# Both halves of the output projection written to a ring of three PSUM banks

## The chip, the cores and the metric

The kernel runs on one core of a Trainium2 chip. The core has a matrix engine (TensorE, PE in the profile; its weight loads are the row PEld), VectorE (DVE), ScalarE (ACT), GpSimd (POOL) and SyncE (SP), which only issues transfers. Each engine works through its own queue in order, and semaphores make it wait for others. Matrix products can be written only to PSUM, which this program divides into eight banks of 128 x 512 float32. The metric is the device time of one execution in microseconds.

## What is computed

The input is 2 sequences of 2048 rows with 256 channels. Each row goes through a layer norm, and from there two branches start:

- a selective state-space layer (Mamba) with an MLP behind it. In short:

```python
xz = rmsnorm(xn) @ in_proj_w.T;  xp, z = split(xz)
xc = silu(conv4(xp) + conv_b)
dt, Bm, Cm = ...                       # from xc
h = h * exp(dt * A) + (dt * xc) * Bm   # a scan over the sequence, 512 channels x 16 states
y = sum_s(h * Cm) + xc * D
x1 = xn + (y * silu(z)) @ out_proj_w.T
s = x1 + silu(rmsnorm(x1) @ mlp_w1.T) @ mlp_w2.T
```

- a mixture of 8 experts of which each row takes its 2 likeliest: a hidden layer of 1024 with relu, a second product back to 256, weighted and summed, then silu; call it `g`.

The output is `x + s * g`. The step that this document is about is `x1 = xn + (y * silu(z)) @ out_proj_w.T`.

## The kernel before

The 4096 rows are cut into 8 blocks of 512 (c = 0 to 7), the 512 channels into 4 groups of 128 (d = 0 to 3), and the 16 states into 8 pairs (g = 0 to 7). The main loop has 8 x 4 x 8 = 256 steps, one for each (c, d, g). In a step VectorE multiplies the input by B (L1498) and runs two scans of 512 (L1502), ScalarE makes the exponentials two steps ahead (L1387), GpSimd multiplies by C (L1430), in most steps adds the two states of the pair (L1432), and TensorE sums the results into a bank for `y` through an identity matrix (L1400), three steps later.

**A planner in Python writes the order.** Each step has two ticks. In each tick the loop emits its own work, then `later.run()` emits what has come due, then `draw` emits filler work for TensorE worth about 1.93 us. The filler comes from generators in lists of falling rank: `pre`, `zs` (the gate projections of `z`), `projs` (the output projections), `chain` (the projections for the next block) and `side` (the expert and MLP tiles). A generator that yields "wait" is passed over for the rest of the tick, and the next list is asked.

**`later` is a list of work with due times.** `later.put(work, frees, after=n)` puts work, such as the step that empties a PSUM bank, n ticks ahead. Whoever wants a bank calls `bank(tag, ...)`, and that calls `later.free`: if the earlier user of the bank has not yet been emitted to its end, everything due up to that end is emitted now, ahead of its time. The chip's engines then wait for each other by semaphores.

**The banks.** Two banks hold the pair of inputs to the scans, one holds dt x xc, one `y`, one has the tag "o" and three have the tag "h". The single bank "o" holds the second product of an expert or MLP tile, and the output projection. The ring of three, "h", holds the conv inputs (px, L621), the small projections (pxd L666, pd L685), the gate projections (pz, L772), the hidden products of the tiles (phe and phm, L946), the transposes (pxse and pxsm, L934), and the scratch output of the squares (sq, L863).

**Expert and MLP tiles** (`Ffn.run`). A tile makes four pairs of hidden products, then waits for `held` to be empty, takes "o", puts its name into `held`, makes 8 second products (poe or pom, L958), clears `held` and calls `finish`. For an expert `finish` plans one add (ys, L1066) two ticks later. For an MLP tile it plans an add (L1218) and behind it a group of three steps (L1228, L1229, L1230, output xom), for which the tanh of the weighted experts (ScalarE, L1207) must be there; its GpSimd sum (L1203) must come before that. An MLP tile's hidden products go through a silu on ScalarE (hidm, L1144), which needs another table than the exponentials (table loads, L183).

**The output projection** (`out_proj(c)`). It is put into `projs` when block c + 1 begins. It loads two halves of `xn`, waits until the last channel group's gated `y` (the product sz, L1408) has been emitted, and then makes two halves of 16 matmuls each (po, L821). For each half it plans an add (L855, result xnr) two ticks later, two squares (L863) and a store to DRAM (L870). When both are made, `projected` lets the gate projections d = 1 to 3 of the next block go. For block 7 (`last`) the first three channel groups are made ahead of time, the first half in "o" and the second in "h".

Of the kernel before, what the change touches and what calls it, by code (L numbers as in the profile page):

```python
# [14 lines left out]
NB, L, DM = 2, 2048, 256  # L15
# [3 lines left out]
P = 128  # L19
# [9 lines left out]
JS = TS // P  # L29
# [23 lines left out]
def kernel(  # L53
# [126 lines left out]
    def act_table(name):  # L180

        if table[0] != name:
            nc.scalar.preload_act_table_set(name)  # L183
            table[0] = name
# [86 lines left out]
    moff, rstd, both_norms, _, _, off = (stat[:, 2 + n, :] for n in range(6))  # L271
# [88 lines left out]
    def can(tag, bufs):  # L360

        n = count.get(tag, 0)
        return n < bufs or n - bufs in gone.get(tag, ())

    def take(tag):
        n = count[tag] = count.get(tag, 0) + 1
        return n - 1

    def drop(tag, n):
        gone.setdefault(tag, set()).add(n)  # L370
# [3 lines left out]
    held = []  # L374

    def ring(tag, bufs):

        n = take(tag)
        later.free(tag, n - bufs)
        return tag, n  # L380

    def bank(tag, shape, name):
        n = ring(tag, 3 if tag == "h" else 1)
        pool = ps_h if tag == "h" else ps_1
        return pool.tile(shape, F32, tag=tag, name=name), n
# [422 lines left out]
    def out_proj(c):  # L808
        last = c == NBLK - 1
        halves = []  # L810
        for hf in range(2):
            while not can("xs", 2):
                yield "wait"
            nx = take("xs")
            xn = rows.tile([P, JS, DM], F32, tag="xs", name=f"xnr{c}_{hf}")
            nc.sync.dma_start(xn, xnd[c][:, ts(hf, JS), :])
            halves.append((hf, xn, nx))
        def product(po, hf, d):

            for j in range(JS):  # L820
                nc.tensor.matmul(  # L821
                    po[:, j, :], szs[c, d][:, ts(hf * JS + j, P)], ow_sb[:, d, :],
                    start=(d == 0 and j == 0), stop=(d == ND - 1 and j == JS - 1),
                )

        pos = []
        if last:

            while (c, ND - 2) not in y_made or held:
                yield "wait"  # L830
            for hf in range(2):
                pos.append(bank("h" if hf else "o", [P, JS, DM], f"po{c}_{hf}"))
                for d in range(ND - 1):
                    product(pos[hf][0], hf, d)
                yield 3 * MM
        while (c, ND - 1) not in y_made:
            yield "wait"
        for hf, xn, nx in halves:
            while (held and not last) or (last and not can("x1", 2)):
                yield "wait"  # L840
            if last:
                po, n = pos[hf]
                product(po, hf, ND - 1)
            else:
                po, n = bank("o", [P, JS, DM], f"po{c}_{hf}")
                for d in range(ND):
                    product(po, hf, d)
            x1 = xn
            if last:
                n1 = take("x1")  # L850
                x1 = rows.tile([P, JS, DM], F32, tag="x1", name=f"x1l{hf}")
                x1_last.append((x1, n1))

            def add(po=po, xn=xn, x1=x1):
                nc.vector.tensor_tensor(x1, po, xn, ALU.add)  # L855

            def squares(hf=hf, x1=x1):
                if last:
                    act_table(WITH_LN)
                sq, ns = bank("h", [P, JS, DM], f"sq{c}_{hf}")  # L860
                for j in range(JS):
                    i = c * J + hf * JS + j
                    nc.scalar.activation(  # L863
                        sq[:, j, :], x1[:, j, :], AF.Square, accum_out=rms[:, 0, i : i + 1],
                    )
                drop(*ns)

            def store(hf=hf, xn=xn, nx=nx):
                if not last:
                    nc.sync.dma_start(x1d[c][:, ts(hf, JS), :], xn)  # L870
                drop("xs", nx)
                if last:
                    root(c, hf)
                elif hf and c == NBLK - 2:
                    root(c)

            later.put(add, n, after=1 if last else 2)
            later.put(squares, after=2 + hf if last else 3)
            later.put(store, after=3 + hf if last else 4)
            yield MM if last else 4 * MM  # L880
        projected.add(c)

    def root(c, hf=None):

        i0, i1 = (c * J, (c + 1) * J) if hf is None else (c * J + hf * JS, c * J + (hf + 1) * JS)
        engine = nc.gpsimd if hf is None else nc.vector
        ss, ms, r, tmp = (rms[:, n, i0:i1] for n in range(4))
        engine.tensor_scalar(ms, ss, 1.0 / DM, RMS_EPS, ALU.mult, ALU.add)
        act_table(WITH_LN)
        nc.scalar.activation(r, ms, AF.Ln)  # L890
        nc.scalar.activation(r, r, AF.Exp, scale=-0.5)
        newton(engine, r, ms, tmp)
        ready_blocks.update((c, h) for h in range(2) if hf in (None, h))
# [577 lines left out]
    for n in range(NS):  # L1471
        c, d, g = at[n]
# [12 lines left out]
        if c > 0 and d == 0 and g == 0:  # L1485
            projs.append(out_proj(c - 1))
        if n == NS - 4:
            projs.append(out_proj(NBLK - 1))
# [97 lines left out]
```

## Time and profile before

| | |
|---|---|
| median of 3 runs | 1489.96 us (1489.83 to 1492.37) |
| profiled execution | 1505.4 us, its span 1503.7 us |
| mean granted clock of TensorE | 0.944 |
| TensorE busy | 1347.4 us (90%) |
| VectorE busy | 1217.2 us (81%) |
| GpSimd busy | 1188.3 us (79%) |
| ScalarE busy | 978.5 us (65%), of it 121 table loads 155.2 us |
| matmuls of the output projection | 256, 61.0 us |

The output projections of the eight blocks begin at 322.8, 470.8, 635.3, 782.5, 937.0, 1105.7, 1309.5 and 1430.4 us of the span. Expert tiles run from about 165 to 1052 us, MLP tiles from there to the end.

In the lists, a bracket such as `[1.94 <-DVE ys L1066]` means that the engine stood idle for 1.94 us before the instruction, and that the wait was ended by the step on VectorE that wrote `ys`, at line 1066. A timeline gives start and duration of neighbouring instructions of one kind, merged. The granted clock is the share of full speed that TensorE was allowed.

### The profile page before, as it was taken

To read this page: it belongs to the slowest core of one execution; us is meant where nothing else is said; L and a number is where in the kernel's file an instruction comes from. 1 tells how busy PE (TensorE), PEld (TensorE's weight loads), DVE (VectorE), ACT (ScalarE), POOL (GpSimd) and SP (SyncE) were. 2 spreads that over 40 slices of the span, in tenths; PEclk is the share of its full clock that TensorE was granted. 3 is DMA by queue.
4 is the path that set the end of the run, shared out by engine and by line. 5 is a ranking of instruction groups with operands and counts; after the bars stand their busy time and mean duration, and the time that the engine had idled before them with its cause. 6 is when DMAs were issued, how large, how long until landed. Compare 5 with 4: busy or idle time off the path is not lost.

```text
span 1503.7 us, 18025 instructions
## 1 busy us (share of the span) xinstructions
PE 1347.4 (90%) x5122; PEld 944.1 (63%) x5122; DVE 1217.2 (81%) x1351; ACT 978.5 (65%) x1765; POOL 1188.3 (79%) x964
## 2 busy tenths in 40 slices
PE   5744799999999999999999999979878998999958
PEld 4531467765776677766776677546655666667726
DVE  7448888889798998799888988999767967888853
ACT  4742777458655776568656865677648988778932
POOL 2665779987898799968997899889975888777860
PEclk9556899999999999999999999999999999999989
DMA  5568134962477345924492449445830116412110
GB/s 187 198 234 304 46 99 145 306 220 76 125 230 280 92 131 180 335 95 121 158 363 74 129 140 331 167 139 175 268 114 8 55 53 211 139 53 60 57 57 14
DMA packets 169317, 231.85 MB, mean 154 GB/s; under 512 B 19825, under 2 KB 139761, under 8 KB 169217
## 3 DMA queue, kind: packets, MB, share of 16 engines
q1 hardware_dynamic: 163072, 213.91, 42.9%
q0 software_dynamic: 6144, 16.79, 3.4%
q8 instruction: 41, 0.67, 0.2%
q14 instruction: 60, 0.48, 0.1%
HBM read 195.12 MB, written 35.52 MB: 153 GB/s over the span
## 4 chain that ended last, share of the span: by engine, by line
PE 44%; POOL 25%; DVE 10%; ACT 10%; issue 6%; DMA 4%; another core or an unknown queue 1%; POOLq 0%; DVEq 0%; SPq 0%; ACTq 0%
POOL h L1430 13%; PE phe L946 9%; PE y L1400 8%; PE poe L958 8%; POOL h L1432 6%; PE pom L958 4%; PE phm L946 4%; PE po L821 3%; ACT L183 2%; PE px L621 2%; DVE h L1502 2%; DMA B<-bcd 2%; ACT da L1387 2%; PE pz L772 2%; DMA C<-bcd 1%
## 5 line engine op out<-in xcount | busy, mean ns | idle before, releaser
L1430 POOL TENSOR_TENSOR h<-h,C 128x1024 f32<-128x1024 f32 x255 | 604.1, 2371 | 36.7 <-issue 11.5
L1502 DVE TENSOR_TENSOR_SCAN h<-da,hs,b 128x512 f32<-128x512 f32 x384 | 477.6, 1270 | 41.4 <-PE y L1400 10.8
L1387 ACT ACTIVATE da<-dt,a_neg 128x512 f32<-128x512 f32 x512 | 352.8, 717 | 93.3 <-DVE h L1502 87.2
L1400 PE MATMUL y<-h,ident 128*128 128x512 f32 x596 | 307.3, 617 | 34.6 <-POOL h L1432 17.5
L1498 DVE TENSOR_TENSOR b<-du,B 128x1024 f32<-128x1024 f32 x256 | 315.0, 1231 | 18.4 <-DMA B<-bcd 9.1
L1432 POOL TENSOR_TENSOR h<-h 128x512 f32<-128x512 f32 x214 | 275.4, 1287 | 16.8
L946 PE MATMUL phe<-xsTe,w_e 128*128 128x256 f32 (+1 forms) x1248 | 268.1, 366 | 9.4 <-ACT xsTe L937 7.6
L946 PEld LDWEIGHTS phe<-xsTe,w_e 128*128 128x128 f32 x1248 | 225.4, 194 | 72.7 <-issue 27.6
L958 PE MATMUL poe<-w_e,hide 128*128 128x256 f32 x1136 | 265.2, 380 | 2.5 <-ACT hide L1053 2.5
L958 PEld LDWEIGHTS poe<-w_e,hide 128*128 128x128 f32 x1136 | 213.8, 190 | 65.1 <-issue 33.5
L1053 ACT ACTIVATE hide<-phe,b 128x256 f32<-128x256 f32 (+1 forms) x312 | 123.6, 450 | 140.8 <-PE phe L946 140.4
L1400 PEld LDWEIGHTS y<-h,ident 128*128 128x128 f32 x596 | 112.2, 197 | 124.0 <-issue 60.5
L1502 DVE TENSOR_TENSOR_SCAN h<-da,b 128x512 f32<-128x512 f32 x128 | 151.3, 1210 | 12.7 <-PE y L1400 4.8
L183 ACT ACT_TABLE_LOAD x121 | 155.2, 1283 | 2.9 <-PEq L1573 0.8
L946 PE MATMUL phm<-xsTm,w_m 128*128 128x256 f32 x512 | 121.0, 387 | 2.7 <-ACT hidm L1144 2.0
L1424 POOL COPY hs<-h 128x2 f32<-128x2 f32 x192 | 42.0, 219 | 100.9 <-DVE h L1502 89.4
L958 PE MATMUL pom<-w_m,hidm 128*128 128x256 f32 x512 | 121.0, 386 | 0.0
L946 PEld LDWEIGHTS phm<-xsTm,w_m 128*128 128x128 f32 x512 | 99.1, 194 | 29.6 <-issue 10.8
L958 PEld LDWEIGHTS pom<-w_m,hidm 128*128 128x128 f32 x512 | 98.5, 194 | 25.2 <-issue 12.5
L462 POOL DMA_INDIRECT xs_d<-xt,slot x64 | 64.0, 1000 | 49.1 <-issue 21.4
L646 DVE SCALAR_TENSOR_TENSOR xc<-px,par_sb,xc 128x512 f32<-128x512 f32 x96 | 71.6, 748 | 30.4 <-ACT xc L638 25.6
L1185 POOL DMA_INDIRECT yk<-ys_d,row_y x60 | 58.3, 972 | 22.6 <-issue 14.2
(221 smaller groups left out, 1366.7 us busy)
## 6 DMA issues: line engine op xcount, KB each, us to landing
w_e<-in_w SPq DMA_DIRECT2D x312, 256.0 KB
B<-bcd SPq DMA_DIRECT2D x64, 512.0 KB
C<-bcd SPq DMA_DIRECT2D x64, 512.0 KB
xs<-xs_d SPq DMA_DIRECT2D x32, 256.0 KB
ys_d<-ys SPq DMA_DIRECT2D x32, 256.0 KB
b<-in_b SPq DMA_DIRECT2D x39, 128.0 KB
xnr<-xnd SPq DMA_DIRECT2D x16, 256.0 KB
xom<-in_x SPq DMA_DIRECT2D x16, 256.0 KB
```

Of the source, the lines that this page charges most:

```text
L183: nc.scalar.preload_act_table_set(name)
L462: r = nc.gpsimd.indirect_dma_start(out=xs_d, out_offset=bass.IndirectOffsetOnAxis(ap=slot[:, k, i : i + 1], axis=0), in_=x_of(i // J, i % ...
L646: nc.vector.scalar_tensor_tensor(v[:, s : s + T], px, conv_w[:, d, KC - 1 - s : KC - s], v[:, s : s + T], ALU.mult, ALU.add,)
L946: nc.tensor.matmul(ph[:, q, :], self.w1[c0 // 2][:, k, ts(q, P)], self.xT[:, k, :], start=(k == 0), stop=(k == KM - 1),)
L958: nc.tensor.matmul(po[:, j, :], self.hid[c // 2][:, c % 2, ts(j, P)], self.w2[c // 2][:, c % 2, :], start=(c == 0 and j == 0), stop=(c == ...
L1053: nc.scalar.activation(hc[:, q, :], ph[:, q, :], AF.Relu, bias=self.b1[:, c0 + q : c0 + q + 1])
L1387: nc.scalar.activation(das[n][:, q, :], dts[c, d], AF.Exp, scale=a_neg[:, d, 2 * g + q : 2 * g + q + 1])
L1400: nc.tensor.matmul(ys[c, d], ident, hts[n][:, q, :], start=False, stop=(g == DS // 2 - 1 and q == nq - 1),)
L1430: engine.tensor_tensor(hts[n], hts[n], bct[c, "C", g], ALU.mult)
L1432: nc.gpsimd.tensor_tensor(hts[n][:, 0, :], hts[n][:, 0, :], hts[n][:, 1, :], ALU.add)
L1498: nc.vector.tensor_tensor(inp, dus[c, d].unsqueeze(1).to_broadcast([P, 2, T]), bct[c, "B", g], ALU.mult,)
L1502: nc.vector.tensor_tensor_scan(hts[n][:, q, :], das[n][:, q, :], inp[:, q, :], 0.0 if c % CPB == 0 else hs[c - 1][:, d, 2 * g + q : 2 * g ...
```

## The change

In `out_proj` of blocks 0 to 6 both halves ask for a bank of the ring "h" instead of "o", and neither waits for `held` any longer. The lines for block 7 stay: its first half keeps "o", and the wait for `held` ahead of it (L829) is not touched.

```diff
         while (c, ND - 1) not in y_made:
             yield "wait"
         for hf, xn, nx in halves:
-            while (held and not last) or (last and not can("x1", 2)):
+            while last and not can("x1", 2):
                 yield "wait"
             if last:
                 po, n = pos[hf]
                 product(po, hf, ND - 1)
             else:
-                po, n = bank("o", [P, JS, DM], f"po{c}_{hf}")
+                po, n = bank("h", [P, JS, DM], f"po{c}_{hf}")
                 for d in range(ND):
                     product(po, hf, d)
```

## The prediction

> **What bounds the kernel now.** I read the engine totals and the 40 slices first, then the stretches of 50 us, then the TensorE groups, and last the timelines around each output projection.
>
> The totals and the slices of the page:
>
> ```profile
> PE 1347.4 (90%) x5122; PEld 944.1 (63%) x5122; DVE 1217.2 (81%) x1351; ACT 978.5 (65%) x1765; POOL 1188.3 (79%) x964
> ...
> PE   5744799999999999999999999979878998999958
> ```
>
> TensorE is the engine to watch: from slice 6 to the end of the 26th it is a row of nines. The answer by stretches gives 735.87 us busy of the 750 us from 200 to 950 (14.1 us idle in all), and 295.51 of the 314 from 1116 to 1430. In the first of these stages an idle microsecond of TensorE is a microsecond of the end; around 1100 it is one only if nothing else is late.
>
> The groups of TensorE, output projection only (columns: busy us, mean ns | idle us before them, and what ended it):
>
> ```profile
> L821 PE MATMUL po<-ow_sb,sz 128*128 128x256 f32 x256 | 61.0, 393 | 16.4 <-DVE xom L1230 10.6 <-DVE ys L1066 3.5 <-DVE xnr L855 1.6
> ```
>
> All three names are work that empties the single bank: the end of an MLP tile (xom), the end of an expert tile (ys) and the projection's own first half (xnr). The timeline places them by block. Here is block 5, TensorE and then VectorE:
>
> ```profile
> 1095.98 3.62 PE L958 MATMUL pom<-w_m,hidm 128*128 128x256 f32 x16
> 1105.74 5.79 PE L821 MATMUL po<-ow_sb,sz 128*128 128x256 f32 x16 [6.15 <-DVE xom L1230]
> 1112.31 3.72 PE L821 MATMUL po<-ow_sb,sz 128*128 128x256 f32 x16 [0.78 <-DVE xnr L855]
> ```
>
> ```profile
> 1099.64 0.67 DVE L1408 SCALAR_TENSOR_TENSOR sz<-y,sz 128x512 f32<-128x512 f32 x1
> 1100.23 0.69 DVE L1218 TENSOR_TENSOR pom<-pom,x1m 128x512 f32<-128x512 f32 x1
> 1103.37 0.70 DVE L1228 SCALAR_TENSOR_TENSOR pom<-yk,pom 128x512 f32<-128x512 f32 x1 [2.46 <-ACT yk L1207]
> ...
> 1111.57 0.69 DVE L855 TENSOR_TENSOR xnr<-po,xnr 128x512 f32<-128x512 f32 x1 [4.78 <-PE po L821]
> ```
>
> The operand of the projection (sz, L1408) is ready at 1100.3, but the bank only at 1105.6, since asking for it makes the planner put the MLP's four closing steps ahead. Then VectorE itself stands 4.78 us, because the add is put into its queue before the product exists. The same pairs elsewhere on TensorE:
>
> ```profile
> 322.78 3.72 PE L821 MATMUL po<-ow_sb,sz 128*128 128x256 f32 x16 [1.94 <-DVE ys L1066]
> ...
> 470.76 3.72 PE L821 MATMUL po<-ow_sb,sz 128*128 128x256 f32 x16 [0.39 <-DVE ys L1066]
> ...
> 786.93 3.72 PE L821 MATMUL po<-ow_sb,sz 128*128 128x256 f32 x16 [0.78 <-DVE xnr L855]
> ...
> 936.98 3.72 PE L821 MATMUL po<-ow_sb,sz 128*128 128x256 f32 x16 [1.18 <-DVE ys L1066]
> ...
> 1309.54 3.69 PE L821 MATMUL po<-ow_sb,sz 128*128 128x256 f32 x16 [3.21 <-DVE xom L1230]
> ```
>
> Block 2 (635.28) shows no wait. The stall total of blocks 0 to 6 is 1.94 + 0.39 + 0.78 + 1.18 + 6.15 + 0.78 + 3.21 = 14.43 us. The remaining 2 us of the 16.4 are the last block's, which the diff leaves as they are.
>
> **The change part by part.** No instruction is added or taken away: 16 matmuls a half, one add, two squares, one store stay. No DMA is added; the loads of xn are still asked for at the start of out_proj, ahead of the waits. SP's store of the half (L870) waits for the add, and behind it stand the next loads of the MLP (xom at 1117.16 after the store of 1112.29); an earlier add lets them go earlier. GpSimd's queue is passed by nothing. What changes is the place of the two halves in TensorE's queue, and the bank.
>
> *The waits for the bank that go.* What is late next is the operand sz, so each wait is cut only to that. Block 0: sz done at 308.3, all 1.94 goes. Block 1: sz ends at 469.44 + 0.67 = 470.11, TensorE is free at 470.37, all 0.39 goes. Block 3: the second half no longer waits for the first one's add, 0.78 goes. Block 4: sz ends at 936.60 and the products could start at about 936.65 instead of 936.98, 0.33 goes. Block 6: sz ends at 1297.0, TensorE free at 1306.33, all 3.21 goes. Block 5: the first half could start at 1100.45, so 5.29 goes, and 0.78 of the second. Its first half also ran slow: 5.80 us in the chain for 16 matmuls that take 3.72 elsewhere, with a granted clock of 0.67 between 1106 and 1112; 2.08 more if the idle time no longer drops the clock. That makes 8.15. But GpSimd had 10.94 us of work in the 18 us from 1098 to 1116, so no more than 7.06 can be won there before it is the bound; I take 7.0. Sum: 1.94 + 0.39 + 0.78 + 0.33 + 7.0 + 3.21 = 13.65 us.
>
> *VectorE's forced adds.* The idle times of VectorE before these adds and before ys and pom (4.78, 2.46, 4.34 in blocks 5 and 6) go or shrink, because the add now comes two steps of the planner later. In blocks 0 to 4 VectorE is 656 us busy of 750, so I cost this at nothing; cover is TensorE's work, and without that cover it would be a further gain.
>
> *An earlier place.* In blocks 0 and 6 the operand was ready 14 and 12 us before the products began, and the planner held them back until the tile ended. Now they go into the middle of the tile's second products. Total work is unchanged and the tile ends two halves (7.4 us) later, so after it both orders stand at the same place. The three later gate projections pz, which wait for out_proj in the planner, come earlier by the same. What is queued behind: TensorE's next tile, whose weights are loaded ahead. Zero, between -1 and +1 us a block.
>
> *Two more takers of the ring of three.* Only block 7's second half uses this ring in the trace, at a time when little else does, so I bound the cost. From below: nothing, since the first half takes a bank last used by a pair of hidden products or a transpose, already emptied by ScalarE (in block 5: hidm at 1090.62 and the sz step at 1095.17, both before 1100). The fourth product after it, some 3.7 + 1.7 + 1.7 us behind its end, needs its add, which comes two planner steps later (about 4 to 5 us). From above: the longest wait of TensorE for this ring near an out_proj, px for DVE xc L646 at 1144.03, 3.92 us. Nearest row: the first hidden products after block 1's projection, which wait 0.55 us for the squares that use the same ring. I take half of it in each of seven blocks, 1.9 us; ends 0 and 7 x 3.92 = 27.4.
>
> **Sum.** 13.65 - 1.9 = 11.7 us less. The profiled execution was 1505.4 us (span 1503.7), the median is 1489.96, a factor of 0.9897; 1493.7 x 0.9897 = 1478.4 us.
>
> **The rivals.**
>
> *Slower: the ring runs short.* Hidden products, px, pz, pd, transposes, squares and now both halves share three banks. If, in the seven blocks, the product behind the halves must wait for an add or for taps as px did at 1144 (3.92), the loss is 27.4 against 13.65: 1519.2 x 0.9897 = 1503.5 us. It decides from 13.65 / 7 = 1.95 us a block. For it: that wait is real. The clock goes with it: px ran its four matmuls in 3.68 instead of 1.88 us after it, at a granted clock of 0.79 between 1142 and 1150, while the 3.21 us at 1306 were followed by 1.00. The Trainium skill, "TensorE: Matmul & The Clock Gate", "What's actually happening", says that the clock falls to half after about one idle window of 3.4 us and needs about as long at work to return; the trace agrees on both sides of that limit. By this rule each wait of 3.92 would cost another 3.4 / 2 = 1.7 us, an estimate, and this rival would end at 1515.3 us instead of 1503.5; the forecast, whose waits stay under a microsecond, would not move. Against it: 200 to 950 shows TensorE with 14.1 us idle in all, with the squares on this ring already, and the release times above leave some 2 us. The Trainium skill, "Perfetto Trace Analysis", "Optimization Strategy", reads a gap that repeats on the engine that should be busy as a sign that room for the next tile can be short. This rival is that rule turned on the ring of three; in this trace the gap repeats at the single bank, and at the ring it shows 3.92 once, which is why the rival gets less than half the forecast's chance.
>
> *No change.* From 756 on, the chain of waits runs through GpSimd's products more than through TensorE, and after block 5 TensorE stands at 1144 for ScalarE in any case. If blocks 0 to 5 give nothing back and only block 6 does, 3.21 - 1.9 = 1.3 us: 1504.1 x 0.9897 = 1488.7 us.
>
> *More.* No ring wait at all, the full 14.43 + 2.08 = 16.5 us: 1488.9 x 0.9897 = 1473.6 us. Against it: the wait for sz remains in blocks 4 and 5.
>
> **How the numbers follow.** The forecast 0.62, more 0.06, no change 0.12, the short ring 0.20. Faster 0.68, within 0.2% (3 us, about what can be told from no change) 0.12, slower 0.20. The forecast alone reaches from 1474 to 1486 (ring cost 0 to 8). The range takes in the no-change case, most of the larger gain and the first third of the slower case: 1471 to 1496.
>
> **What would show it.** Right: L821 loses xom and ys as releasers except in block 7 (1.19 there stays), the idle before it falls from 16.4 to 2 to 5 us, block 5's halves take 3.7 us each, and the halves of blocks 0 and 6 lie inside a tile's second products. Wrong: the idle before phe, phm, px and pz (9.4, 2.7, 5.9 and 0.7) grows by more than 13 with DVE xnr or ACT sq as releaser. The prediction fails too if GpSimd or ScalarE fills the stretch at 1098 to 1116, so that its 18 us stay.

## The result and the profile after

The changed kernel takes 1477.07 us (median of 4 runs, 1475.81 to 1477.73) against 1491.16 us of before: a ratio of 0.9901, 95% interval 0.9889 to 0.9913. On another chip it was 0.9883 (0.9863 to 0.9903): 1488.6 against 1504.41 us. The ratio is an estimate of its own and not the quotient of the two medians, which would be 0.9906 and 0.9895. The time of the first 110 us differs from chip to chip and from run to run: the first product of the y groups begins at 99.8 us in one trace and at 119.5 in another. So runs on different chips are compared by their ratios here, and traces by markers behind that stretch.

The totals and the slices of the page of the changed kernel:

```profile
PE 1337.3 (91%) x5122; PEld 937.0 (63%) x5122; DVE 1214.0 (82%) x1351; ACT 979.8 (66%) x1767; POOL 1186.6 (80%) x964
...
PE   5843999999999999999999999988898998999958
```

The same number of matmuls, 10 us less of busy time, and a span of 1475.6 instead of 1503.7 us. Of these 28.1 us, 11.2 lie ahead of the first place where the two programs differ. Now TensorE's groups of the changed kernel (busy us, mean ns | idle us before, and what ended it): the output projection, and the takers of the ring that could have inherited its waits.

```profile
L946 PE MATMUL phe<-xsTe,w_e 128*128 128x256 f32 (+1 forms) x1248 | 266.5, 365 | 11.1 <-ACT xsTe L937 7.5 <-ACT hide L1053 2.0 <-DVE xc L646 1.0
L946 PE MATMUL phm<-xsTm,w_m 128*128 128x256 f32 x512 | 121.5, 389 | 4.2 <-ACT hidm L1144 3.5 <-ACT xsTm L937 0.7
L821 PE MATMUL po<-ow_sb,sz 128*128 128x256 f32 x256 | 57.6, 380 | 2.0 <-DVE xom L1230 1.2 <-DVE sz L1408 0.8
L621 PE MATMUL px<-xrTr,in_sb 128*128 128x512 f32 x96 | 47.1, 614 | 5.9 <-DVE xc L646 3.9 <-ACT hide L1053 2.0
L1396 PE MATMUL y<-xc,ddiag 128*128 128x512 f32 x64 | 34.4, 620 | 7.8 <-DVE sz L1408 7.8
```

The 16.4 us before L821 are 2.0, all of it block 7's. Its busy time fell by 3.4 us, 2.4 of it in block 5, where no half runs at a low clock any more (7.07 us for both instead of 5.79 and 3.72). Of the others, phe has 1.7 us more than before (9.4), phm 1.5 more (2.7), px the same 5.9, and the first product of a new y group, which waits for sz, 3.4 more (4.4). A second trace of the same kernel (e0) has phe at 9.9, phm at 2.7 and the y group at 7.4, so of these only the last repeats. It is mostly two new waits, 1.78 and 1.21 us, after projections 0 and 2, which start early. The waits did not simply move to the ring.

Block 5 on TensorE, and on VectorE, in the changed kernel:

```profile
1081.87 3.62 PE L958 MATMUL pom<-w_m,hidm 128*128 128x256 f32 x16
1085.32 7.07 PE L821 MATMUL po<-ow_sb,sz 128*128 128x256 f32 x32
1092.23 1.02 PE L1396 MATMUL y<-xc,ddiag 128*128 128x512 f32 x2
```

```profile
1085.57 0.67 DVE L1408 SCALAR_TENSOR_TENSOR sz<-y,sz 128x512 f32<-128x512 f32 x1
...
1087.34 0.67 DVE L1218 TENSOR_TENSOR pom<-pom,x1m 128x512 f32<-128x512 f32 x1
...
1090.48 0.67 DVE L855 TENSOR_TENSOR xnr<-po,xnr 128x512 f32<-128x512 f32 x1
1091.06 0.68 DVE L1228 SCALAR_TENSOR_TENSOR pom<-yk,pom 128x512 f32<-128x512 f32 x1
...
1094.38 0.67 DVE L855 TENSOR_TENSOR xnr<-po,xnr 128x512 f32<-128x512 f32 x1
```

The two halves follow the tile's last products without a gap. The MLP's closing steps stand at their due places among the scans, and VectorE waits for none of the lines shown. Note the first line: the projection begins 0.25 us before sz has even been started. Of its four channel groups only the last reads this sz.

**Where the time went.** Take as a marker the first product of a y group (y<-xc) in the last channel group of each block, and measure from that of block 0, which lies before any difference. Between the markers of two blocks stands one output projection. Saved us against the trace of before (the columns e1 to e11 are experiments, described below):

| stretch | forecast, before ring waits | whole change | e1 wait kept | e5 one bank | e4 squares off the ring | e11 one bank, squares off |
|---|---|---|---|---|---|---|
| projections 0 and 1 | 2.3 | 0.4 | 1.8 | -0.3 | 1.9 | 2.5 |
| projections 2 and 3 | 0.8 | 1.0 | 1.3 | 1.9 | 0.9 | 2.2 |
| projection 4 | 0.3 | 1.6 | 0.2 | -1.4 | 3.1 | 1.0 |
| projection 5 | 7.0 | 9.0 | 10.6 | 11.9 | 9.5 | 11.7 |
| projection 6 | 3.2 | 6.2 | 3.4 | 7.1 | 6.2 | 5.1 |
| from there to the end | 0 | -1.2 | -0.8 | -2.0 | -1.1 | -1.9 |
| sum | 13.65 | 16.9 | 16.5 | 17.1 | 20.4 | 20.6 |

A single trace wanders: in e2, whose blocks 0 to 4 are those of before, one marker stands 2.8 us off and the next ones 1.7. In e3, whose blocks 5 to 7 are those of before, projection 5 shows 2.3, projection 6 -0.9 and the rest -0.9. So the losses of about 1 us in the last row belong to the trace of before and not to the edits. The second trace of the changed kernel (e0) has 10.8 at projection 5, 5.3 at projection 6 and a sum of 16.0. A cell of 1 or 2 us means little; projections 5 and 6 and the sums mean something.

### The profile page after: what moved, and what is told of

Its sections match the earlier page's. It is cut to its first block, busy times and chain, and to the rows that moved or that the text cites. A ratio compares the mean times of both kernels' runs of the same rounds, so it can differ in the third digit from the quotient of the medians.

```text
span 1475.6 us, 18038 instructions
## 1 busy us (share of the span) xinstructions
PE 1337.3 (91%) x5122; PEld 937.0 (63%) x5122; DVE 1214.0 (82%) x1351; ACT 979.8 (66%) x1767; POOL 1186.6 (80%) x964
## 4 chain that ended last, share of the span: by engine, by line
PE 35%; POOL 23%; ACT 7%; DVE 5%; issue 4%; DMA 1%; SPq 0%; POOLq 0%; DVEq 0%; ACTq 0%
POOL h L1430 12%; PE y L1400 7%; PE phe L946 6%; POOL h L1432 5%; PE poe L958 5%; PE pom L958 5%; PE phm L946 4%; PE po L821 2%; ACT L183 2%; DVE h L1502 2%; PE pz L772 2%; POOL dt L713 1%; PE px L621 1%; POOL ls L712 1%; POOL yk L1185 1%
## 5 line engine op out<-in xcount | busy, mean ns | idle before, releaser
L1430 POOL TENSOR_TENSOR h<-h,C 128x1024 f32<-128x1024 f32 x255 | 603.8, 2370 | 33.0 <-DVE h L1502 9.4
L958 PE MATMUL pom<-w_m,hidm 128*128 128x256 f32 x512 | 119.5, 382 | 0.0
L646 DVE SCALAR_TENSOR_TENSOR xc<-px,par_sb,xc 128x512 f32<-128x512 f32 x96 | 71.6, 748 | 27.8 <-ACT xc L638 23.9
```

Source lines behind the costliest of these rows:

```text
L646: nc.vector.scalar_tensor_tensor(v[:, s : s + T], px, conv_w[:, d, KC - 1 - s : KC - s], v[:, s : s + T], ALU.mult, ALU.add,)
L958: nc.tensor.matmul(po[:, j, :], self.hid[c // 2][:, c % 2, ts(j, P)], self.w2[c // 2][:, c % 2, :], start=(c == 0 and j == 0), stop=(c == ...
L1430: engine.tensor_tensor(hts[n], hts[n], bct[c, "C", g], ALU.mult)
```

## Experiments

**The whole change again, beside others (e0).** The changed kernel, unedited.

> The whole change, unedited, beside the other runs on one chip. By the first comparison 0.990 of before; by the markers of the two traces, without the start, 16.9 us less. If keeping the wait is as good as dropping it, this run lies within 2 us of that kernel's 0.9888; if the early start pays, it is below by 2 to 4 us (block 6 gives 5.6 instead of 3.6 us).

Measured: 0.9883 (0.9863 to 0.9903). This is the figure for the comparisons below. It and the next one cannot be told apart: the "2 to 4 us below" of the early start did not show.

**Bank alone (e1).** The halves go to the ring, but still wait for the tile.

```diff
-            while last and not can("x1", 2):
+            while (held and not last) or (last and not can("x1", 2)):
```

> Both halves in the ring of three, but they still wait until no tile holds the single bank. Theory (the loss was the forced emptying of the single bank, not the late start): the stalls of 14.4 us at the projections still go, block 5 gains about 9.5 us as with the whole change, and the time is 12 to 15 us below before, within 2 us of the changed kernel. Rival (the early start in the middle of a tile is what pays): only the blocks whose projection begins at the same place, 1, 3, 4 and 5, gain, some 11 us, and block 6 keeps its 3.2 us wait or loses the 5.6 us that it won; the time is 4 to 6 us above the changed kernel.

Measured: 0.9888 (0.9874 to 0.9902), as fast as the whole change. Its group of TensorE:

```profile
L821 PE MATMUL po<-ow_sb,sz 128*128 128x256 f32 x256 | 57.7, 380 | 2.0 <-DVE xom L1230 1.2 <-DVE sz L1408 0.8
```

The same 2.0 us as with the whole change. So the earlier place in the middle of a tile, the second half of the description, brings nothing that can be told in sum: by the table projection 6 gains 2.8 from it and projections 0 and 1 lose 1.4, and the other differences, at 4 and 5, are no larger than those between two traces of one kernel. The rival's figure, 4 to 6 us above the changed kernel, does not fit: the ratios differ by 0.7 us and the marker sums by 0.5.

**Neither bank nor early place (e5).** The single bank stays; out_proj no longer has it emptied ahead of time, but yields until its turn.

```diff
-            while (held and not last) or (last and not can("x1", 2)):
+            while (not last and (held or not can("o", 1))) or (last and not can("x1", 2)):
```

> The single bank stays, but out_proj no longer forces its emptying: it yields until the step that frees the bank has come due, for each half. Theory (the loss is the forced order, steps put into VectorE's queue before their inputs exist): 8 to 13 us below before, though no bank was added. Rival (one bank is too few, whatever the order): the halves now wait two or three ticks more and the next tile's second products wait for the bank behind them; within 3 us of before, or slower.

Measured: 0.9884 (0.9870 to 0.9899), 16.6 us below before by medians, more than the 8 to 13 expected. Block 5 of this kernel, TensorE and VectorE:

```profile
1096.71 3.62 PE L958 MATMUL pom<-w_m,hidm 128*128 128x256 f32 x16
1100.17 5.34 PE L946 MATMUL phm<-xsTm,w_m 128*128 128x256 f32 x24
...
1108.78 3.62 PE L821 MATMUL po<-ow_sb,sz 128*128 128x256 f32 x16
...
1113.95 3.62 PE L821 MATMUL po<-ow_sb,sz 128*128 128x256 f32 x16
```

```profile
1102.18 0.68 DVE L1218 TENSOR_TENSOR pom<-pom,x1m 128x512 f32<-128x512 f32 x1
...
1105.31 0.67 DVE L1228 SCALAR_TENSOR_TENSOR pom<-yk,pom 128x512 f32<-128x512 f32 x1
...
1112.43 0.69 DVE L855 TENSOR_TENSOR xnr<-po,xnr 128x512 f32<-128x512 f32 x1 [1.08 <-PE po L821]
```

While the bank is being emptied, the planner gives TensorE the hidden products of the next tile (phm), and the closing steps stand among the scans. Its groups of TensorE:

```profile
L821 PE MATMUL po<-ow_sb,sz 128*128 128x256 f32 x256 | 58.6, 382 | 4.5 <-DVE ys L1066 1.8 <-DVE xom L1230 1.2 <-DVE sz L1408 0.8
L621 PE MATMUL px<-xrTr,in_sb 128*128 128x512 f32 x96 | 45.5, 596 | 0.0
```

One bank was enough. What cost 14 to 17 us was the order: asking for the bank put its emptying into VectorE's queue before the inputs existed, and the products behind it. The equal time is a balance, though. Here 2.5 us of waits for the bank stay in blocks 0 to 2 and phe waits 4.4 us more than before (13.8), while the 5.9 us before px are gone.

**Block 5 alone (e2).**

```diff
-            while (held and not last) or (last and not can("x1", 2)):
+            while (held and not last and not (c == 5)) or (last and not can("x1", 2)):
...
-                po, n = bank("o", [P, JS, DM], f"po{c}_{hf}")
+                po, n = bank("h" if c == 5 else "o", [P, JS, DM], f"po{c}_{hf}")
```

> The change in block 5 alone. By the two traces block 5 gave 9.0 to 9.6 us of the sum, so 9 to 10 us below before. If the cap of the prediction held (GpSimd's 10.94 us of work in that stretch), no more than 7.0 us. If what is won there is lost to other engines before the end, under 3 us.

Measured: 0.9938 (0.9925 to 0.9951), which is 7.4 to 11.3 us of 1505.3; by its markers 9.6 us at projection 5, of which 7.7 are left at the end. By medians it is 8.2. The cap of 7.0 lies just outside the interval. One of seven projections holds more than half of the gain.

**Blocks 0 to 4 alone (e3).** The same two lines with `c < 5`.

> The change in blocks 0 to 4, where TensorE is 98% busy. The prediction's terms for these blocks sum to 3.4 us (1.94, 0.39, 0, 0.78, 0.33) less 1.4 us of ring waits: about 2 us below before. The markers of the two traces give 0.4, 0, -0.1, 1.1 and 1.4: 2.8 us. If a short ring eats it: no change or slower.

Measured: 0.9989 (0.9978 to 1.0), 2.1 us by medians and about as expected. Five projections in the stage where TensorE is 98% busy give little, because their waits were short; they don't cost anything either.

**Fewer takers of the ring (e4).** The squares of blocks 0 to 6 write their scratch output into the half's own bank, so each half takes one bank of the ring and not two.

```diff
-            def squares(hf=hf, x1=x1):
+            def squares(hf=hf, x1=x1, po=po, n=n):
...
-                sq, ns = bank("h", [P, JS, DM], f"sq{c}_{hf}")
+                if last:
+                    sq, ns = bank("h", [P, JS, DM], f"sq{c}_{hf}")
+                else:
+                    sq, ns = po, n
...
-            later.put(add, n, after=1 if last else 2)
+            later.put(add, n if last else None, after=1 if last else 2)
```

> The whole change, and the squares write their scratch output into the half's own bank instead of taking another one of the ring: two takers of the ring fewer in each of seven blocks, each half's bank held a tick longer. Theory (the ring of three has room): within 1.5 us of the whole change. Rival (the ring is short and eats part of the gain, the 1.9 us that the prediction set aside and more): 2 to 5 us below the whole change.

Measured: 0.9865 (0.9842 to 0.9887), and again, on another chip:

> The same kernel as before with the squares in the half's own bank, beside the next two on one chip. 0.9865 of before then; by the markers of its trace 20.4 us less. The same again within 0.3%.

Measured: 0.9866 (0.9845 to 0.9888). Medians lie 3.4 us below the whole change run beside it, and the markers say 3.5. The intervals of the ratios overlap, but the two measurements agree, and so do their traces (20.4 and 20.7 by the markers): the ring did eat some of the gain. Both traces put it at projections 0, 1 and 4.

**A longer hold (e8).** The add of each half two ticks later than in the changed kernel.

```diff
-            later.put(add, n, after=1 if last else 2)
-            later.put(squares, after=2 + hf if last else 3)
-            later.put(store, after=3 + hf if last else 4)
+            later.put(add, n, after=1 if last else 4)
+            later.put(squares, after=2 + hf if last else 5)
+            later.put(store, after=3 + hf if last else 6)
```

> The whole change, with the add of each half planned four ticks after its products instead of two (squares and store after it likewise), so that each bank of the ring is held some 4 to 5 us longer. If the margin of the ring is the 2 us that the prediction worked out, later takers force the add out ahead of its time or wait for it, 1 to 3 us in each of seven blocks: 7 to 20 us above the whole change. If there is ample room: within 2 us of it.

Measured: 0.9937 (0.9912 to 0.9961), 7.3 us above the whole change, at the low end of what was expected if the margin is small. TensorE and VectorE groups of this kernel:

```profile
L621 PE MATMUL px<-xrTr,in_sb 128*128 128x512 f32 x96 | 48.2, 627 | 8.7 <-DVE xc L646 6.8 <-ACT hide L1053 1.9
L646 DVE SCALAR_TENSOR_TENSOR xc<-px,par_sb,xc 128x512 f32<-128x512 f32 x96 | 71.6, 748 | 32.8 <-ACT xc L638 29.6 <-ACT xc L631 0.8
```

The wait of px for the ring grew from 3.9 to 6.8, and VectorE stood 32.8 us before the taps (L646), which empty px's bank, instead of 27.8. The 2.9 us are a single wait behind projection 5, 6.77 us instead of 3.92. The markers show 3.5 us for the whole, 2.5 of it at projection 5. The execution in the trace took 1492.38 us, 3.5 less than the median of 1495.92 (1491.52 to 1500.52); what the longer ones lose on top is not located.

**No forced emptying of the ring (e7).** In the changed kernel, px, pz, hidden pairs and the halves yield until their bank of the ring is free in due time.

```diff
+            while not can("h", 3):
+                yield "wait"
             project(d)
...
-        while d and c and c - 1 not in projected:
+        while (d and c and c - 1 not in projected) or not can("h", 3):
             yield "wait"
...
             for c0 in range(0, NH, 2):
+                while not can("h", 3):
+                    yield "wait"
                 self.pair(c0)
...
             else:
+                while not can("h", 3):
+                    yield "wait"
                 po, n = bank("h", [P, JS, DM], f"po{c}_{hf}")
```

> The whole change, and every filler that can wait (px, pz, hidden pairs, both halves) yields until its bank of the ring has come free by its due time, instead of forcing the bank's emptying. Theory (forced emptying is what costs): the remaining forced steps, such as the taps that VectorE waits for (25.6 us of idle time before them, mostly off the path), come later; 0 to 10 us below the whole change. Rival: the other filler runs short while several wait, ticks are left empty, TensorE's work slips to the end: 5 to 30 us above.

Measured: 0.9885 (0.9865 to 0.9906), and its markers agree with those of the whole change within 0.1 us all along. These takers hardly ever force anything, so there was nothing to win by this. Other takers, such as the squares, cannot yield and can still force; that was not tried here.

**Wait kept in blocks 0 to 4, squares off the ring (e10).**

```diff
-            while last and not can("x1", 2):
+            while (held and c < 5) or (last and not can("x1", 2)):
```

on top of the edit of e4.

> The squares off the ring, and blocks 0 to 4 keep the wait for the tile while 5 to 7 start early. By the markers the early start costs 1.4 us in block 0 and brings 1.6 in block 6 on the full ring. If the cost in block 0 is the early start itself, 1 to 1.5 us below the kernel without the wait; if it came from the ring alone, which the squares have left, no difference (within 0.7 us).

Measured: 0.9868 (0.9845 to 0.9890), the same median as the kernel without the wait, 1486.64 us. By the markers projections 0 and 1 give 1.8 against 1.9 us. On the full ring it was 1.8 with the wait (e1) and 0.4 without. So the early start loses there only while the squares are on the ring; with fewer takers it costs nothing.

**One bank, squares off the ring (e11).** The edit of e4 on e5.

> The single bank, emptied in due time, with the squares written into it: the ring of three loses two takers in a block and gains none. If the takers of the ring were what cost after the forced emptying is gone, 2 to 4 us below the kernel that waits for the single bank in due time (0.9884), as low as the other two. If the single bank, now held a tick longer by each half, binds: 0 to 5 us above it.

Measured: 0.9856 (0.9832 to 0.9880), the lowest median of the three on this chip, 1484.84 us (1484.29 to 1485.41) against 1486.64 of e4 and e10. The difference of 1.8 us lies inside the intervals. Against e5 it is 4.2 us less by the ratios, whose intervals overlap, and 3.5 by the markers; 2 to 4 were expected. Its group of px:

```profile
L621 PE MATMUL px<-xrTr,in_sb 128*128 128x512 f32 x96 | 45.2, 593 | 0.0
```

The 5.9 us before px, which before and the changed kernel share, are gone. They were already gone in e5, and e4, which only takes the squares off the ring, keeps them. So this part comes from emptying the single bank in due order, and the 3.5 us on top, by the markers, from the squares. The kernel takes nothing from the ring that before did not take, and gives two takers back.

## Why the prediction came out right

The time lay in the range, 1.3 us from the forecast, but part of that nearness is luck, two errors that met: the gain was 14.1 us by medians instead of the 11.6 that 11.7 x 0.9897 makes, and before itself ran 1.2 us longer beside it than the 1489.96 it started from. By ratio the gain was 0.99% and 1.17% against the 0.79% forecast; by the markers 16.9 us against 11.7.

- *The waits that go, 14.43 us.* Right as a mechanism and nearly whole: L821's idle time fell from 16.4 to 2.0.
- *"What is late next is the operand sz, so each wait is cut only to that."* Wrong, in blocks 4 and 5. Only the last quarter of a half's products reads the last sz; the first twelve can go. In block 4 the first half begins 0.3 us before that sz is started, and the block gave 1.6 by the markers instead of 0.33; in block 5 TensorE has no gap at all.
- *Block 5, capped at 7.0 by GpSimd's work.* The term that was mis-sized: 9.0 us in the trace, 10.8 in e0's and 9.6 in e2. The uncapped sum of the waits and the clock, with the whole 6.15, is 6.15 + 0.78 + 2.08 = 9.01. GpSimd's 10.94 us of work in the old stretch need not all be done in the new one. In the changed kernel's answer for that stretch, GpSimd (the last of the five busy times) is nearly full, and the rest of the work follows behind it:

```profile
1084.00:1092.40 8.40, 8.40 (x40) 7.39 (x40) 8.03 (x10) 4.47 (x10) 8.16 (x7) 1.00 0.05 19
```

  For GpSimd itself the cap was right. Measured from the marker of block 0, its product (L1430) that stood at 1102.88 comes 2.9 us earlier, and the one that stood at 1116.22 comes 9.8 us earlier: 6.9 us won, against the 7.06 worked out. On TensorE the gain goes from the same 2.9 us to 12.5 at the end of the two halves, 9.6 us. GpSimd makes up the difference by its product of 1138.83 (12.5 us earlier), in a stretch where it had stood waiting before. Two of its waits in the trace of before:

```profile
1115.95 0.19 POOL L1424 COPY hs<-h 128x2 f32<-128x2 f32 x1 [5.14 <-DVE h L1502]
...
1128.81 0.19 POOL L1424 COPY hs<-h 128x2 f32<-128x2 f32 x1 [1.27 <-DVE h L1502]
```

- *The low clock of block 5, 2.08 us.* Right: the two halves are busy 2.4 us less, and the granted clock is 1.00 here.
- *Block 6, 3.21 us.* Too low. 6.2 came in the trace, of it about 2 from two later waits of TensorE that also shrank: pz for hidm (0.72 before, none after) and the transposes for xrm (1.56 before, 0.35 after). With the tile still awaited (e1) the block gave 3.4, and both waits were back (0.54 and 1.56). But e5, which waits for the tile too and has the single bank, gave 7.1 with neither wait. So this part hangs on where the halves fall in the order, not on the early start as such; what sets it was not isolated.
- *An earlier place, "zero, between -1 and +1 us a block".* Right in sum, as e1 shows, though single blocks went beyond: about 1.4 us lost at projections 0 and 1, where px and pz came earlier and a y group waited 1.78 us for sz, and 2.8 more than with the wait (e1) at projection 6.
- *Two more takers of the ring, 1.9 us.* The prediction took this for the cost of the halves. No run isolates that cost. e4 frees two other takers in a block and wins 3.5, which is of the same order and far from the 27.4 of the rival. In the trace, the new direct wait is phe for xc, 1.0 us; it stands in e2 too, ahead of that kernel's only edit, so it is not the halves'. The wait of px (3.9) was there before. The margin is thin, as it was worked out to be: two ticks more cost 7.3 us by medians (e8), of which the trace shows half.
- *The rivals.* The short ring is refuted as the deciding case and confirmed as a small one. The no-change rival expected the chain to hold elsewhere; block 5 alone gave 9.6 us, of which 7.7 reached the end (e2). The case of more gain (16.5) is nearer to the markers' 16.9 than the forecast was; by the medians of the first comparison (14.1) the gain lies halfway between the two.
- *The clock, "the trace agrees on both sides of that limit".* It agrees at the two gaps named, of 3.92 and 3.21 us, but not throughout: the same trace has a gap of 2.03 us with a low clock behind it, as the last section shows. No term of the sum hangs on it, only the 1515.3 us of the short ring.
- What the prediction did not ask was which part of the change works. It took the waits for a lack of banks; e5 shows that they were a matter of order. The wait of px (3.92 at 1144), which it took as a sign of a short ring, is gone in e5 too, with the same three banks and the squares still on them.

## What to carry to other kernels

When a wait for a single buffer shows up on the busiest engine, look at how its emptying got into the other queue before adding a buffer: here, yielding until the emptying was due was worth as much as moving both halves to a ring of three. If a group accumulates over several operands, ask which of its instructions needs the late one; a start time goes by the first, not by the last. And a cap made from another engine's work in a stretch holds only for what the end of the stretch needs, as work that may lag goes past it.

## What the runs showed of the hardware

The clock did not follow the length of the gap alone. After the same 2.03 us of idleness, at the same place of the program, px ran in 3.45 us before and in 1.98 us after. The granted clock was 0.83 and 0.74 in the stretches from 964 to 968 and 968 to 972 us before, and 1.00 in those from 950 to 954 and 954 to 958 us after. From the two traces, before and after:

```profile
966.26 3.45 PE L621 MATMUL px<-xrTr,in_sb 128*128 128x512 f32 x4 [2.03 <-ACT hide L1053]
```

```profile
952.30 1.98 PE L621 MATMUL px<-xrTr,in_sb 128*128 128x512 f32 x4 [2.03 <-ACT hide L1053]
```

So a gap well below the 3.4 us that the prediction quoted from the Trainium skill ("TensorE: Matmul & The Clock Gate", "What's actually happening") was followed by a low clock in one execution and not in the other. Ten of the traces have this gap, and another of 3.92 us before px behind projection 5. After the shorter one, px took 1.98 to 1.99 us in six of them, 2.66 and 2.90 in e4 and its repetition, and 3.40 and 3.45 in e0 and before. After the longer one it took 3.38 to 3.78 us in eight, 2.40 in e10, and 1.98 in the repetition of e4, where the granted clock stayed at 1.00 from 1122 to 1134 us. What decides was not tried. At these two places it made 0 to 1.8 us, which is enough to move a cell of the table.
